# A graph network's attention layers: sums over eight tiles in a span of 72 nodes, masks made once, chains in one array

## The chip, the cores and the metric

The kernel runs on one core of one Trainium2 chip. Five engines work beside each other: TensorE (PE; its weight loads are shown as PEld), VectorE (DVE), ScalarE (ACT), GpSimd (POOL) and SyncE (SP). Each runs its own queue of instructions in order and waits for the others by semaphores. The metric is the time of one execution on the device in microseconds (us), as the median of several runs. A profile is a further execution, recorded by the hardware profiler.

## The reference

`x` has 6250 nodes of 128 values. There are 100000 edges; `dst` is sorted, and drawn as 6250 u^2 with u uniform, so low nodes have many edges and high nodes few.

```
dst = minimum((6250 * uniform(100000) ** 2.0).astype(int32), 49999);  sort by dst
h = relu(layernorm(x))
h = rgcn(h, basis1, ...); h = rgcn(h, basis2, ...)      # 16 relations, 8 bases
x = x + h
h = relu(layernorm(x))
for each of two attention layers:
    src, dst with a self loop for every node            # 106250 entries
    xw = h @ W                                          # 4 heads of 32
    e = leaky_relu(al_s[src] + al_d[dst], 0.2)
    alpha = exp(e - max over the node's entries) / (sum over the node's entries)
    out[n] = sum over the entries of n of alpha * xw[src]
    h = elu(batchnorm(out + b))
x = x + h
```

All values are float32.

## The kernel before

**Tiles.** Edges are packed with their target into sortable keys. For the attention layers the self loops are merged in (`gat_list`), which gives 106250 sorted entries, filled up to 832 tiles (NT) of 128. Eight tiles (SC) make one row of the sorted array, 1024 entries on end; 32 tiles (TC) make a chunk, and there are 26 chunks (NCH). Each entry's target node lies in `dst`, a column for each tile.

**Two relational layers** (`edge_layer`, `rgcn`) come first. They gather a row for each edge from a table in HBM, tile by tile. While the first of them runs, a generator, advanced by one step in each of 98 half groups, builds the lists of the attention layers: `gat_list`, then `windows`, then `chains`.

**Windows and passes.** A sum over the entries of a tile is a matmul with a selection: for entry e and place w of a span of nodes it has 1 where the entry's target is the span's first node plus w. `windows` stores for each tile its first node (`base`) and for each entry its distance from it (`ahead`). It also counts how many spans are needed: L353 to L357 compare the widest distance with the steps 0, W, 2W, ..., and the number of steps that aren't above it is `passes`. `layer` (L606) runs the whole attention layer in a loop of so many passes; each pass moves all spans on by W (24 nodes), through `offset` (L614) and `start` (L616). An entry that lies outside the span of a pass adds nothing in it.

**An attention layer** (`gat`, L962) goes through the chunks:

- `gathers(k + 1)`: 32 indirect DMAs from POOL's queue (L584), each with 128 rows of 136 values (128 of the node and its 8 attention values), into two row buffers of 16 tiles. The pool `grp` has 7 such buffers (L1134).
- `sums(k)`: it weights the rows in place (L917, four tiles at a time), makes a selection for every eight tiles (L601), one matmul for each tile (L937: rows as the weights, 24 columns moving), and one addition for each tile into the accumulator at a place that is read from a register (L921). Registers are loaded by `registers` (L589), 16 at a time. Ahead of it a column that two chunks share is corrected (L930, L931).
- `softmax(k + 1)`: written as a generator and woven into the steps of `sums(k)`. An edge's logit, the running maximum and the sum are taken along the 128 entries of a tile with scans (L806, L830, L831, L836, L837), with masks that say where a new node begins (`cut` L789, `same` L791). A node may go on from tile to tile, so the ends of the tiles are linked by scans over the 32 tiles of a chunk in four partitions, one for each head (L814, L852, L854, L874, L877); three values are carried over to the next chunk.

The order of each engine is that of the program text (`in_order`). Scores are turned around by PE (L799, L905), and copied by ACT (L797, L908).

**Between and after** the attention layers, `bn_elu` normalises, with tiles from the same pool `grp`, and makes the next layer's table, or the output.

Of the kernel before, what the change touches and what calls it, by code (L numbers as in the profile page):

```python
# [10 lines left out]
BF16 = mybir.dt.bfloat16  # L11
AF = mybir.ActivationFunctionType
# [32 lines left out]
NZ = -(-(N + 1) // W)  # L45
WG = 288
# [5 lines left out]
BIG = 1e30  # L52

# [14 lines left out]
class Gnn:  # L68
# [251 lines left out]
    order = staticmethod(lambda v: v.rearrange("o (c p) -> o p c", p=NP))  # L320
    by_tile = staticmethod(lambda v: v.rearrange("o (p c) -> o p c", c=SC))

    def windows(self, scratch):

        nc, const, dst = self.nc, self.const, self.dst
        order, by_tile = self.order, self.by_tile
        self.base = const.tile([1, NT], I32, name="base")
        nc.vector.tensor_copy(by_tile(self.base), order(dst[0:1, :]))  # L330
        self.ahead = const.tile([P, NT], F32, name="ahead")
        last, firsts, lasts = scratch[:, :NT], scratch[:, NT:2 * NT], scratch[:, 2 * NT:3 * NT + 1]
        flags = scratch[:, 4 * NT:6 * NT].rearrange("o (i t) -> o i t", i=2)
        for c in range(0, NT, NT // 2):
            w = slice(c, c + NT // 2)
            ps = self.ps()[:, :NT // 2]
            nc.tensor.matmul(ps, self.ones, dst[0:1, w], start=True, stop=True)
            nc.vector.scalar_tensor_tensor(self.ahead[:, w], ps, -1.0, dst[:, w], op0=ALU.mult, op1=ALU.add)
            ps = self.ps()[:, :NT // 2]
            nc.tensor.matmul(ps[:1, :], self.ident[:, P - 1:P], dst[:, w], start=True, stop=True)  # L340
            nc.vector.tensor_copy(last[:, w], ps[:1, :])
        yield
        nc.vector.tensor_copy(by_tile(firsts), order(dst[0:1, :]))
        nc.vector.memset(lasts[:, 0:1], -1.0)
        nc.vector.tensor_copy(by_tile(lasts[:, 1:]), order(last))
        nc.vector.tensor_tensor(flags[:, 0, :], firsts, lasts[:, :NT], ALU.is_equal)
        nc.vector.tensor_tensor(flags[:, 1, :], firsts, lasts[:, 1:], ALU.is_equal)

        nc.vector.tensor_sub(lasts[:, 1:], lasts[:, 1:], firsts)
        widest = scratch[:, 0:1]  # L350
        nc.vector.tensor_reduce(widest, lasts[:, 1:], AX.X, ALU.max)
        steps = self.small.tile([1, NZ], F32, name="steps", bufs=1)
        nc.vector.tensor_scalar(steps, self.steps, widest, None, op0=ALU.is_le)  # L353
        count = self.small.tile([1, 1], F32, name="count", bufs=1)
        nc.vector.tensor_reduce(count, steps, AX.X, ALU.add)
        passes = const.tile([1, 1], I32, name="passes")
        nc.vector.tensor_copy(passes, count)  # L357
        self.passes_g = passes
        yield

        self.both = const.tile([H, 2, NT], BF16, name="both")
        for i in range(2):
            for c in range(0, NT, NT // 2):
                w = slice(c, c + NT // 2)
                ps = self.ps()[:, :NT // 2]
                nc.tensor.matmul(ps[:H, :], self.ones[:, :H], flags[:, i, w], start=True, stop=True)
                nc.vector.tensor_copy(self.both[:, i, w], ps[:H, :])
        yield

    def chains(self, scratch):  # L370

        nc, const = self.nc, self.const
        chunked = lambda t: t.rearrange("h (k t) -> h k t", t=TC)
        link, one = chunked(self.both[:, 0, :]), chunked(self.both[:, 1, :])
        self.link = link
        wide = [H, NCH, TC + 1]

        self.linkpen = const.tile(wide, BF16, name="linkpen")
        nc.vector.memset(self.linkpen, -BIG)
        lk = chunked(scratch[:H, NCH * P:NCH * P + NT])  # L380
        nc.vector.tensor_scalar(lk, link, 1.0, BIG, op0=ALU.subtract, op1=ALU.mult)
        nc.vector.tensor_copy(self.linkpen[:, :, :TC], lk)
        yield


        self.through = const.tile(wide, BF16, name="through")
        nc.vector.memset(self.through, 0.0)
        nc.vector.tensor_mul(self.through[:, :, 1:], link, one)
        self.throughpen = const.tile(wide, BF16, name="throughpen")
        nc.vector.tensor_scalar(self.throughpen, self.through, 1.0, BIG, op0=ALU.subtract, op1=ALU.mult)  # L390
        yield

        self.back = const.tile(wide, BF16, name="back")
        nc.vector.memset(self.back, 0.0)
        nc.vector.tensor_mul(self.back[:, :, :TC - 1], one[:, :, :TC - 1], link[:, :, 1:])
        self.apart = const.tile([H, NCH, TC], BF16, name="apart")
        nc.vector.tensor_scalar(self.apart, one, -1.0, 1.0, op0=ALU.mult, op1=ALU.add)
        self.backpen = const.tile(wide, BF16, name="backpen")
        nc.vector.memset(self.backpen, -BIG)
        nc.vector.tensor_scalar(self.backpen[:, :, :TC], one, 1.0, BIG, op0=ALU.subtract, op1=ALU.mult)  # L400
        nc.vector.tensor_add(self.backpen[:, :, :TC - 1], self.backpen[:, :, :TC - 1], self.linkpen[:, :, 1:TC])
        yield


        self.rows = const.tile([P, NCH, P], F32, name="rows")
        ri = scratch[:, :NCH * P].bitcast(I32).rearrange("p (k e) -> p k e", e=P)
        kv = self.keys[:NT * P].rearrange("(k t e) -> t k e", t=TC, e=P)
        for h in range(H):
            nc.sync.dma_start(ri[h * TC:(h + 1) * TC], kv)
        for k in range(0, NCH, 2):  # L410
            yield
            nc.vector.tensor_scalar(ri[:, k:k + 2], ri[:, k:k + 2], KDST, None, op0=ALU.logical_shift_right)
            nc.vector.tensor_scalar_mul(self.rows[:, k:k + 2], ri[:, k:k + 2], BIG)

        self.rowlink = const.tile([P, NCH], F32, name="rowlink")
        for k in range(NCH):
            yield
            self.spread(self.rowlink[:, k:k + 1], lk[:, k, :])
# [13 lines left out]
    def own_tile(self, out, v):  # L432

        nc = self.nc
        t = self.small.tile([P, TC], F32, name="spread")
        nc.vector.tensor_mul(t, v, self.tile_of)
        nc.vector.tensor_reduce(out, t, AX.X, ALU.add)

    def spread(self, out, v):

        ps = self.ps()
        self.nc.tensor.matmul(ps[:, :TC], self.of_head, v, start=True, stop=True)
        self.own_tile(out, ps[:, :TC])
# [149 lines left out]
    def bases(self, t0):  # L593

        return self.registers(self.start[0:1, t0 // G, :])

    def selections(self, t0):

        s = self.sel.tile([P, GD, W], F32, name="sel")
        c = column(t0)  # L600
        self.nc.vector.tensor_tensor(  # L601
            s, self.window[:, None, :].to_broadcast([P, GD, W]),
            self.offset[:, c:c + (GD - 1) * NP + 1:NP, None].to_broadcast([P, GD, W]), ALU.is_equal)
        return s

    def layer(self, body):  # L606
# [3 lines left out]
        passes = nc.values_load(self.passes_g, min_val=1, max_val=NZ,  # L610
                                skip_runtime_bounds_check_because="a step of 0 is at most any width")
        self.in_order()
        with self.tc.For_i(0, passes):
            nc.vector.tensor_scalar(self.offset, self.ahead, self.moved, None, op0=ALU.subtract)  # L614
            groups = self.base.rearrange("o (g t) -> o g t", t=G)
            nc.vector.tensor_scalar(self.start, groups, self.moved[0:1, :], float(N), op0=ALU.add, op1=ALU.min)  # L616
            nc.vector.tensor_copy(self.leads, self.base[:, ::TC])
            body()
            nc.vector.tensor_scalar_add(self.moved, self.moved, float(W))
# [57 lines left out]
    def rgcn(self, acc, table, bs, wc, others=iter(())):  # L677
# [18 lines left out]
        def select(h):  # L696
            s = self.sel.tile([P, GD, W], F32, name="sel")
            nc.vector.tensor_tensor(s, self.window[:, None, :].to_broadcast([P, GD, W]),
# [78 lines left out]
    def softmax(self, k):  # L777
# [3 lines left out]

        nc, t = self.nc, lambda name: self.soft.tile([P, P], F32, name=name)
        v, carry = self.v[k], self.carry
        dr = self.rows[:, k, :]

        cut = self.soft.tile([P, P + 1], F32, name="cut")
        nc.vector.tensor_copy(cut[:, 0:1], self.rowlink[:, k:k + 1])
        nc.vector.memset(cut[:, P:], 0.0)
        nc.vector.tensor_sub(cut[:, 1:P], dr[:, :P - 1], dr[:, 1:])  # L789
        same = t("same")  # L790
        nc.vector.tensor_scalar(same, cut[:, :P], 0.0, None, op0=ALU.is_equal)  # L791
        yield
# [17 lines left out]
        dl = self.chain.tile([H, TC + 1], F32, name="dl")  # L810
        nc.vector.tensor_copy(dl[:, 1:], cps[:H, :TC])
        nc.vector.tensor_copy(dl[:, 0:1], carry[0])
        dc = self.chain.tile([H, TC + 1], F32, name="dc")
        nc.vector.tensor_tensor_scan(dc, self.through[:, k, :], dl, 0.0, op0=ALU.mult, op1=ALU.add)  # L814
        df = self.chain.tile([H, TC], F32, name="df")
        nc.vector.tensor_mul(df, dc[:, :TC], self.link[:, k, :])
# [4 lines left out]
        self.own_tile(dcol, ps[:, :TC])  # L821
        e = t("e")
        nc.vector.tensor_scalar(e, dr, dr[:, 0:1], dcol, op0=ALU.is_equal, op1=ALU.mult)
        nc.vector.tensor_add(e, e, d)
# [6 lines left out]
        nc.vector.tensor_tensor_scan(m[:, ::-1], cut[:, P:0:-1], fwd[:, ::-1], -BIG, op0=ALU.add, op1=ALU.max)  # L831
# [5 lines left out]
        nc.vector.tensor_tensor_scan(total[:, ::-1], cut[:, P:0:-1], run[:, ::-1], -BIG, op0=ALU.add, op1=ALU.max)  # L837
# [4 lines left out]
        pair = lambda x: x.rearrange("h (i t) -> h i t", i=2)  # L842

        ends = cps[:H, :4 * TC].rearrange("h (j i t) -> h j i t", j=2, i=2)
        ml = self.chain.tile([H, 2, TC + 1], F32, name="ml")
        nc.vector.tensor_copy(ml[:, 0, :TC], ends[:, 0, 0, :])
# [373 lines left out]
```

## Time and profile before

| what | us |
|---|---|
| median of 3 runs (lowest, highest) | 4508.44 (4505.27, 4509.29) |
| the profiled execution | 5581.38 |
| its span, first to last instruction | 5573.1 |
| first relational layer, first gather | 60.8 |
| second relational layer, first gather | 1302.8 |
| first attention layer, first gather | 2588.5 |
| second attention layer, first gather | 4089.2 |
| last gather | 5440.2 |
| mean granted TensorE clock | 0.613 |

The profiled execution is longer than the median run by 1073 us; durations of single instructions come from it. A busy time is the sum of an engine's instructions; idle time before an instruction is put down to what ended it. "Remote" and "another core or an unknown queue" mean that the profile doesn't show what released the wait. Gathers go through the queue `software_dynamic`, 218.57 of 256.84 MB.

### The profile page before, as it was taken

Reading aid. Unit: us, or ns where it says so; the run is one execution under the profiler, and the core shown is the slowest. Engines: PE = TensorE matmul, PEld = TensorE weight load, DVE = VectorE, ACT = ScalarE, POOL = GpSimd, SP = SyncE. Lnnn points to the kernel's source line nnn. Section 1 sums busy time; section 2 is a strip of 40 time slices with the busy share of each in tenths; the row PEclk is TensorE's granted clock in tenths of the full one; section 3 lists DMA queues with packets and bytes.
Section 4 is the critical chain, followed back from the end, with each engine's and each line's share of the span. In section 5 each row is a group of like instructions: output and inputs, shape, how many; then the busy total and the mean of one; then the engine's idle time right before and its main releaser. Section 6 shows DMA issues by size and latency. Waiting matters only on the chain.

```text
span 5573.1 us, 41706 instructions
## 1 busy us (share of the span) xinstructions
PE 2479.0 (44%) x10042; PEld 2106.2 (38%) x10042; DVE 2558.3 (46%) x8572; ACT 475.6 (9%) x683; POOL 3123.3 (56%) x3242
## 2 busy tenths in 40 slices
PE   2666666664666656663133233232412333323334
PEld 1455545553555555552123232232412322322224
DVE  4345555452444444453254444354633444444446
ACT  2011000011010000012000000000020000000002
POOL 4566666654566666633655555655246656555560
PEclk6777777785777777775555555555555555555555
DMA  3121121112122111111211111211021111111110
GB/s 102 49 55 44 45 59 46 46 36 64 50 65 55 47 46 47 47 26 48 48 41 42 39 43 40 46 38 43 17 61 44 44 39 44 42 42 42 39 44 27
DMA packets 135170, 256.84 MB, mean 46 GB/s; under 512 B 56017, under 2 KB 76485, under 8 KB 134916
## 3 DMA queue, kind: packets, MB, share of 16 engines
q0 software_dynamic: 103296, 218.57, 16.6%
q1 hardware_dynamic: 31388, 34.67, 2.0%
q8 instruction: 87, 1.43, 0.1%
q14 instruction: 167, 1.37, 0.1%
q10 hardware_dynamic: 232, 0.80, 0.1%
HBM read 236.45 MB, written 17.37 MB: 46 GB/s over the span
## 4 chain that ended last, share of the span: by engine, by line
another core or an unknown queue 24%; DVE 21%; PE 12%; issue 12%; POOL 4%; DVEq 2%; ACT 1%; DMA 0%; ACTq 0%; SPq 0%; POOLq 0%
PE ps L937 6%; POOL v L584 4%; DVE acc L921 3%; PE ps L740 2%; DVE v L917 2%; DVE part L749 2%; DVEq L589 1%; DVE own L895 1%; DVE own L900 1%; DVE den L884 1%; PE ps L711 1%; PE ps L695 1%; DVE e L901 1%; DVE hot L692 1%
## 5 line engine op out<-in xcount | busy, mean ns | idle before, releaser
L584 POOL DMA_INDIRECT v<-gtable,src_i x1664 | 1628.6, 979 | 1368.4 <-ACT sd L797 537.0
L584 POOL DMA_INDIRECT v<-htable,src_e x1564 | 1486.0, 950 | 948.8 <-issue 447.5
L740 PE MATMUL ps<-sw,v 128*128 128x192 f32 x3128 | 808.7, 423 | 213.2 <-issue 186.8
L937 PE MATMUL ps<-sel,v 128*128 128x24 f32 x3328 | 773.7, 385 | 179.3 <-DVE v L917 72.8
L937 PEld LDWEIGHTS ps<-sel,v 128*128 128x128 f32 x3328 | 748.4, 330 | 228.7 <-issue 90.8
L740 PEld LDWEIGHTS ps<-sw,v 128*128 128x128 f32 x3128 | 715.6, 255 | 270.7 <-issue 235.7
L749 DVE TENSOR_TENSOR part<-part,ps 128x192 f32 x1564 | 552.7, 353 | 362.7 <-remote 201.4
L921 DVE TENSOR_TENSOR acc<-acc,ps 128x24 f32 x1664 | 296.3, 178 | 851.2 <-remote 636.4
L711 PE MATMUL ps<-part,basis 128*128 128x288 f32 x1568 | 419.4, 422 | 7.2 <-DVE part L749 6.9
L695 PE MATMUL ps<-wc,hot 128*128 128x64 f32 x392 | 108.7, 371 | 690.4 <-DVE hot L692 642.2
L892 PE MATMUL ps<-part,of_head 4*128 4x65 f32 x104 | 35.6, 443 | 853.4 <-DVE part L890 704.5
L716 DVE TENSOR_TENSOR acc<-acc,ps 128x288 f32 x98 | 44.6, 455 | 773.4 <-remote 696.8
L706 ACT COPY part<-zero 128x2304 f32<-128x2304 f32 x100 | 210.8, 2110 | 1920.3 <-remote 1598.9
L695 PEld LDWEIGHTS ps<-wc,hot 128*128 128x128 f32 x392 | 82.4, 257 | 749.3 <-DVE hot L692 684.2
L703 DVE TENSOR_TENSOR sw<-sel,ps 128x1536 f32<-128x1536 f32 x196 | 343.7, 1754 | 25.3 <-remote 8.7
L892 PEld LDWEIGHTS ps<-part,of_head 4*128 4x128 f32 x104 | 25.8, 307 | 860.4 <-DVE part L890 709.8
L711 PEld LDWEIGHTS ps<-part,basis 128*128 128x128 f32 x1568 | 302.5, 198 | 86.2 <-issue 8.1
L430 PE MATMUL ps<-sel,head_of 128*4 128x32 f32 x208 | 44.5, 312 | 641.8 <-DVE sel L428 454.2
L917 DVE TENSOR_TENSOR v<-v,w 128x512 f32<-128x512 f32 x416 | 286.3, 688 | 8.6 <-issue 5.9
L430 PEld LDWEIGHTS ps<-sel,head_of 128*4 128x4 f32 x208 | 9.4, 84 | 654.7 <-DVE sel L428 461.4
L691 PE MATMUL ps<-relT,of_tile 8*128 8x128 f32 x392 | 122.7, 402 | 32.0 <-DMA relT<-rels 21.7
L833 ACT ACTIVATE e<-e 128x128 f32<-128x128 f32 x52 | 16.1, 309 | 1301.8 <-DVE e L832 713.4
(293 smaller groups left out, 2061.2 us busy)
## 6 DMA issues: line engine op xcount, KB each, us to landing
v<-gtable,src_i POOLq DMA_INDIRECT x1664
v<-htable,src_e POOLq DMA_INDIRECT x1564
gtable<-gtb SPq DMA_DIRECT2D x14, 476.0 KB
acc<-htable SPq DMA_DIRECT2D x24, 256.0 KB
htable<-x SPq DMA_DIRECT2D x7, 448.0 KB
relT<-rels SPq DMA_DIRECT2D x196, 4.0 KB
htable<-y SPq DMA_DIRECT2D x7, 448.0 KB
x<-in_x_dram SPq DMA_DIRECT2D x7, 441.0 KB
```

The lines of the kernel that those rows point to most:

```text
L584: self.nc.gpsimd.indirect_dma_start(out=out, out_offset=None, in_=table, in_offset=bass.IndirectOffsetOnAxis(ap=idx, axis=0))
L691: nc.tensor.matmul(ps[:, :P], self.of_tile, rel.pop(h), start=True, stop=True)
L695: nc.tensor.matmul(coef[h][:, P:P + SC * NBASE], t, wc.rearrange("p g b -> p (g b)"), start=True, stop=True)
L703: nc.vector.tensor_tensor(x, s[:, :, None, :].to_broadcast(shape), c[:, :, :, None].to_broadcast(shape), ALU.mult)
L706: nc.scalar.copy(x, self.zero[:, :, None].to_broadcast([P, NBASE, WG]))
L711: nc.tensor.matmul(ps[:, :WG], bs[:, b, :], x[:, b, :], start=b == 0, stop=b == NBASE - 1)
L740: nc.tensor.matmul(ps[:, (j - i) * NBASE * W:(j - i + 1) * NBASE * W], v[:, i0 + j, :], sw[h][:, j].rearrange("p b w -> p (b w)"), start=T ...
L749: nc.vector.tensor_add(o, o, x.rearrange("p (b w) -> p b w", b=NBASE))
L892: nc.tensor.matmul(ps[:, :2 * TC + 1], self.of_head, part, start=True, stop=True)
L917: nc.vector.tensor_mul(x, x, wz[:, :, :, None].to_broadcast([P, Q, H, FH]))
L921: nc.vector.tensor_add(o, o, ps[:, j * W:(j + 1) * W])
L937: nc.tensor.matmul(ps[:, j * W:(j + 1) * W], v[i // G][:, i % G, :D], s[:, i % GD, :], start=True, stop=True)
```

## The change

The passes' step becomes WA = 72 nodes, in place of W = 24, and a span now belongs to the eight tiles of one row (1024 entries) and not to one tile. Distances `ahead` are taken from the first node of the row, and the widest distance that sets `passes` is that of the row's last entry. The eight matmuls of a row add up in one PSUM bank (`start` at the first, `stop` at the last), and one addition of 72 columns takes them to the accumulator. Selections are 128 x 8 x 72, and rows are weighted eight tiles at a time. The relational layers keep spans of 24.

The softmax's masks `cut`, `same`, `head` and `tail` are computed for all chunks when the lists are built, and kept in bf16 and bytes. The chains' running values lie in one array `ends` of 2 x 833 for the whole pass, which the next chunk's scan takes up, and the backward ones in two arrays in turn; columns for a tile's first and last node are worked on together. One copy (`shrink`) goes from DVE to ACT. `softmax` has one step less, and isn't advanced at step 3 any longer. `grp` has 6 buffers in place of 7.

The diff, cut to its core:

```diff
+WA = 72
+NZA = -(-(N + 1) // WA)
...
     def windows(self, scratch):
+        ps = self.ps()[:, :NP]
+        nc.tensor.matmul(ps, self.ones, dst[0:1, :NP], start=True, stop=True)
+        nc.vector.tensor_sub(by_place(self.ahead), by_place(dst), ps[:, None, :].to_broadcast([P, SC, NP]))
...
-            nc.tensor.matmul(ps[:1, :], self.ident[:, P - 1:P], dst[:, w], start=True, stop=True)
+            nc.tensor.matmul(ps[:1, :], self.ident[:, P - 1:P], self.ahead[:, w], start=True, stop=True)
             nc.vector.tensor_copy(last[:, w], ps[:1, :])
+        count = self.small.tile([1, 2], F32, name="count", bufs=1)
+        nc.vector.tensor_reduce(count[:, 0:1], last, AX.X, ALU.max)
+        steps = self.small.tile([1, NZA], F32, name="steps", bufs=1)
+        nc.vector.tensor_scalar(steps, self.steps_a, count[:, 0:1], None, op0=ALU.is_le)
+        nc.vector.tensor_reduce(count[:, 1:2], steps, AX.X, ALU.add)
+        self.passes_g = const.tile([1, 1], I32, name="passes")
+        nc.vector.tensor_copy(self.passes_g, count[:, 1:2])
...
     def chains(self, scratch):
         for k in range(0, NCH, 2):
+            z = slice(k, k + 2)
...
+            nc.vector.tensor_sub(self.cut[:, z, 1:P], rows[:, z, :P - 1], rows[:, z, 1:])
+            for mask, e in ((self.head, 0), (self.tail, P - 1)):
+                nc.vector.tensor_tensor(mask[:, z], rows[:, z], rows[:, z, e:e + 1].to_broadcast([P, 2, P]), ALU.is_equal)
-        for k in range(NCH):
+        half = NCH // 2
+        for k in range(0, NCH, half):
             yield
-            self.spread(self.rowlink[:, k:k + 1], lk[:, k, :])
...
+            nc.vector.tensor_scalar(self.same[:, z], self.cut[:, z, :P], 0.0, None, op0=ALU.is_equal)
...
     def layer(self, body):
         with self.tc.For_i(0, passes):
             nc.vector.tensor_scalar(self.offset, self.ahead, self.moved, None, op0=ALU.subtract)
...
             body()
-            nc.vector.tensor_scalar_add(self.moved, self.moved, float(W))
+            nc.vector.tensor_scalar_add(self.moved, self.moved, float(WA))
...
     def softmax(self, k):
-        nc.vector.tensor_sub(cut[:, 1:P], dr[:, :P - 1], dr[:, 1:])
-        nc.vector.tensor_scalar(same, cut[:, :P], 0.0, None, op0=ALU.is_equal)
-        yield
+        cut, same = self.cut[:, k, :], self.same[:, k, :]
...
-        nc.vector.tensor_tensor_scan(dc, self.through[:, k, :], dl, 0.0, op0=ALU.mult, op1=ALU.add)
+        dc = self.ends[:, 0, :]
+        nc.vector.tensor_tensor_scan(dc[:, past], ahead, cps[:H, :TC], dc[:, k * TC:k * TC + 1], op0=ALU.mult, op1=ALU.add)
...
-        for i, c in enumerate((0, P - 1)):
-            self.own_tile(cols[:, i:i + 1], ps[:, i * TC:(i + 1) * TC])
-            nc.vector.tensor_scalar(inv, dr, dr[:, c:c + 1], cols[:, i:i + 1], op0=ALU.is_equal, op1=ALU.mult)
-            nc.vector.scalar_tensor_tensor(e, inv, 1.0, e, op0=ALU.add, op1=ALU.mult)
+        self.own_tile(cols, ps[:, :2 * TC].rearrange("p (i t) -> p i t", i=2))
+        nc.vector.tensor_scalar(inv, self.head[:, k, :], cols[:, 0:1], 1.0, op0=ALU.mult, op1=ALU.add)
+        nc.vector.scalar_tensor_tensor(inv, self.tail[:, k, :], cols[:, 1:2], inv, op0=ALU.mult, op1=ALU.add)
+        nc.vector.tensor_mul(e, e, inv)
...
     def sums(self, k, w, shrink):
-        def add(t, at, ps):
-            for j in range(2):
-                o = self.sum[:, bass.ds(at[(t + j) % G], W)]
-                nc.vector.tensor_add(o, o, ps[:, j * W:(j + 1) * W])
+        def add(i, ps):
+            o = self.sum[:, bass.ds(at[i], WA)]
+            nc.vector.tensor_add(o, o, ps[:, :WA])
...
+        at = self.registers(self.start[0:1, k, :])
...
-            ps = self.ps()
-            for j in range(2):
-                i = t + j
-                nc.tensor.matmul(ps[:, j * W:(j + 1) * W], v[i // G][:, i % G, :D], s[:, i % GD, :], start=True, stop=True)
+            for i in range(t, t + 2):
+                nc.tensor.matmul(ps[:, :WA], v[i // G][:, i % G, :D], s[:, i % GD, :],
+                                 start=i % GD == 0, stop=i % GD == GD - 1)
...
-                if step == 3 or step >= TC // 4 - 1:
+                if step >= TC // 4 - 1:
...
-        self.grp = self.pool("grp", 7)
+        self.grp = self.pool("grp", 6)
```

## The prediction

> **What bounds the kernel now.** I read the page's busy times first, then the groups of the gathers, then what POOL waited for, then POOL in order of time, then four stretches of equal work side by side.
>
> From the page (line, engine, operation, count, then busy us and mean ns):
>
> ```profile
> span 5573.1 us, 41706 instructions
> PE 2479.0 (44%) x10042; PEld 2106.2 (38%) x10042; DVE 2558.3 (46%) x8572; ACT 475.6 (9%) x683; POOL 3123.3 (56%) x3242
> ...
> L584 POOL DMA_INDIRECT v<-gtable,src_i x1664 | 1628.6, 979 | 1368.4 <-ACT sd L797 537.0
> L584 POOL DMA_INDIRECT v<-htable,src_e x1564 | 1486.0, 950 | 948.8 <-issue 447.5
> ```
>
> POOL does nothing but gathers, and is busier than any other engine. The 1664 gathers of the attention layers are 2 x 832: one for each of the 832 tiles in each layer, so each layer's loop ran once. The attention loop's first instruction says so too:
>
> ```profile
> L614 DVE TENSOR_SCALAR offset<-ahead,moved x2: 653/653/653, 2585.2 to 4085.7; 128x832 f32<-128x832 f32 x2
> ```
>
> POOL in order of time, at the end of one run of gathers (start, duration, idle before):
>
> ```profile
> 3077.85 0.94 POOL L584 DMA_INDIRECT v<-gtable,src_i  x1 [0.30 <-issue]
> 3079.10 0.94 POOL L584 DMA_INDIRECT v<-gtable,src_i  x1 [0.30 <-issue]
> 3095.22 1.22 POOL L584 DMA_INDIRECT v<-gtable,src_i  x1 [15.18 <-ACT sd L797]
> 3096.74 0.94 POOL L584 DMA_INDIRECT v<-gtable,src_i  x1 [0.30 <-issue]
> ```
>
> A gather starts every 1.25 us, 40 us for the 32 tiles of a chunk; then, in the profiled execution, POOL waits some 13 to 15 us for a free row buffer. The last table sets two chunks with gathers beside two at the end of the layer without (us, busy time and count of PE, PEld, DVE, ACT, POOL, then clock, DMA share, GB/s):
>
> ```profile
> 3691.80:3744.40 52.60, 17.22 (x77) 15.75 (x76) 24.52 (x108) 1.83 (x8) 31.55 (x32) 0.50 0.19 43
> 3744.40:3797.30 52.90, 17.23 (x77) 15.76 (x77) 24.53 (x108) 1.84 (x8) 31.24 (x32) 0.50 0.19 43
> 3962.60:3991.90 29.30, 17.30 (x77) 15.83 (x77) 24.12 (x108) 1.88 (x8) 0.00 (x0) 0.50 0.00 0
> 3991.90:4021.30 29.40, 17.29 (x77) 15.75 (x77) 24.04 (x108) 1.83 (x8) 0.00 (x0) 0.50 0.00 1
> ```
>
> The same work of DVE and PE takes 29.3 us with POOL quiet and 52.8 us beside gathers, with the same busy times: the difference is waiting.
>
> **Which of these holds in the runs shown.** The profiled execution took 5581 us (span 5573, 8 around it), the median run 4508. I try the gathers alone. Busy 1628.6 + 1486.0, plus 3228 gaps of 0.30, makes 4083 us. In five stretches of the profile POOL has no gather at all: 61 before the first, 83 between the relational layers, 144 ahead of each attention layer and 132 at the end (the wait and idle columns of POOL and the first and last starts of L584), 564 together. 4083 + 564 leaves 926 of the span for waits between gathers. The median run is 1073 below the profiled one. So it has no room for those waits: 4508 - 8 - 4083 = 417 remain for the five stretches, less than their 564. That fits if the layers' ends don't lag as they do here (the last gather of the first attention pass starts at 3944 and its last addition ends at 4039). With ends of about 440 the interval comes to 1.26 us. I take the unprofiled kernel to be paced by the gathers throughout, at 1.26 us each, with DVE and PE hidden below them. This is an inference; the second and third rivals are what follows if it is false.
>
> **The change, part by part.**
>
> *The number of passes.* This decides. A pass adds only edges whose node lies within the span after its start; the loop runs once for every step 0, span, 2 x span ... that isn't above the widest reach. Before, the reach is that of one tile of 128 sorted entries, and the span 24. After, it is that of eight tiles, 1024 entries, and the span 72. Targets are 6250 u^2, so near node n there are 100000 / (2 sqrt(6250 n)) edges a node and one self loop: 9 at the last node. 128 / 9 is 14 nodes, 1024 / 9 is 114. Worked out exactly on the reference's inputs, the widest tile reaches 17 and the widest group 113; 44 of the 104 groups reach 72 or more. 17 is below 24: one pass. 113 is above 72 and below 144: steps 0 and 72 count, so *two passes*, in each of the two attention layers. The body is all inside that loop: 832 gathers, 26 chunks of softmax, the weighting and the sums are done again. The second pass costs at least 832 x 1.26 = 1048 us on POOL. Around it lies a tail in which POOL is idle: landing and softmax of the last chunk, then its sums. The profile has 29.3 us for a chunk without gathers and 17 from the last chunk's weights at 4021.3 to its last addition; less what can start before the last landing (some 10) and what DVE saves below, some 35, and 5 to restart the loop (at 4085.2 to 4089.2 in the profile). I take 40; the ends are 25 and the lagging 94. One more pass: 1088. Two layers: *+2176 us*.
>
> *Sums.* For a chunk, 32 additions at 0.178 become 4 of 128x72, between 0.178 and the 0.29 of a 128x128 one; I take 0.24: -4.7 us. The 4 selections grow from 128x192 (0.35) to 128x576; the 128x512 weighting took 0.69, so 0.75: +1.6. The 8 weightings (5.5) become 4 twice as long (estimate 1.25 each): -0.5. Two register loads, of 16 and one, become one of five: -2 on DVE's queue. PE still runs 32 matmuls, each in two parts, 72 columns wide; rows of 24 and 192 columns take 385 and 423 ns, so nothing.
>
> *Softmax.* Masks computed once take away L787 to L791 (0.73); one array for the chains takes away the copies and memsets of L811, L812, L846 to L849 and L873 to L880 (1.1); the two-fold column work (L436, L437, L900, L901: 2.0) and L823, L824, L888, L890 shrink by about 1.3; the copy L903 goes to ACT, which is busy 1.8 of 52 us. Together some -3. So DVE goes from 24.3 to about 17.5 us a chunk. Beside 40 us of gathers that is worth nothing on the path; without that cover it would be 26 x 7 = 180 us a pass. Only the tails keep it: about -8 for each of the two passes that were there, *-15*.
>
> *Lists.* Cut, head, tail and same are made once, in 15 steps in place of 39: a subtraction and two comparisons of 256 elements for each of 13 (about 0.35 each by the 128x192 row, 14 us), two long comparisons (4), less 26 column spreads of two 0.18 operations (9). +9 on DVE in the first relational layer, where gathers pace it and DVE is busy 77 of 139 us at most: nothing; 9 if uncovered.
>
> *Row buffers, 7 to 6.* A chunk holds two. A gather three chunks ahead now waits for the same half of chunk k to be summed, in place of a half before it; behind it on POOL's queue stand all later gathers, and behind those the next softmax on ACT, PE and DVE. With a chunk of 40 us on POOL and under 29 on DVE, POOL doesn't run ahead and finds buffers free: nothing. In the normalisation stages the same pool serves three tiles a step: 0 to 20 us over both; I take 5.
>
> *Two rules weighed.* The Trainium skill (DMA: Bandwidth & Descriptors, section Anatomy of one DMA) gives a DMA of this kind 2.0 us plus its bytes at 436 GB/s; 128 rows of 544 B make 2.16 us. If gathers stood one after another, the added 1664 would cost 3594 and the sum would be 8080. The trace has one every 1.25 us, since several are in flight; I use the row. The second speaks against the change's longer DVE operations: the skill (SBUF — State Buffer, section Who interferes with whom) says that a DVE operation with two SBUF inputs makes a GpSimd operation that reads SBUF wait for its whole length. The new selections and weightings are 0.7 to 1.25 us long. Taken fully, 8 us a chunk would be added, 830 over four passes, and 7490 in all. The trace has such operations now, 6.9 us a chunk, and its gathers average 978 ns over a median of 945: 1.1 us a chunk. So scaled, 8 us cost 0.2 more: 5 a pass, inside the range.
>
> *Sum.* 4508 + 2176 - 15 + 5 = 6674; I say **6670**, 48% slower. Against the profiled execution's own time: old passes took 1454 (2585.2 to 4038.9) and 1440; a new one lies between 1090 and 1440, so its profile should have 5581 + 2 x 1447 - 4 x (0 to 357), 7050 to 8480, far above the median run as now.
>
> **Rivals.** (1) *One pass after all*: the place is the widest group's reach, and it decides at 72; with 71 or less the loop would run once, and the change would save its two tails and little else: about 4490, faster by 0.4%. The measure of 113 speaks against it. (2) *The old kernel was paced by DVE and PE, and the profiler slows all alike* (4508 / 5581 = 0.81): gathers every 1.02 us, the old pass 1170 or 45 a chunk. The new chunk then falls to about 37 (45 less 7 and a few waits), the pass to 26 x 37 + 40 = 1002: 4508 - 2340 + 4008 = 6180. For it: the 15 us waits of POOL. Against it: it needs gathers a fifth faster than any in the trace. (3) *Delays beside gathers stay*, as 52.8 against 29.3 shows, and the new pass runs at some 45 a chunk: 4508 + 2 x (1170 + 40) = 6930. (4) The change does what it says, and DVE's gain shows: it would need passes under half the old one's, below about 560; the gathers' busy time alone is 814 a pass.
>
> **How the numbers follow.** Paced by gathers, two passes: 0.72, own range 6560 to 6760. Rival 2: 0.13. Rival 3: 0.13. Rival 1: 0.02. The range 6420 to 6800 takes in the tails of 25 to 94, intervals down to 1.15, and parts of rivals 2 and 3. About 0.2% is what a measurement of this kernel can tell from no change. Slower 0.98, faster 0.015, same 0.005.
>
> **What would show it.** In the changed kernel's profile: 3328 gathers from gtable in place of 1664; the offset instruction of the loop 4 times; 6656 records of the summing matmul; 416 additions of 128x72; DVE's busy time a chunk near 17.5 us; chunks without gathers near 22 us at the ends of passes. The prediction is wrong if the offset instruction appears twice (rival 1), or if gathers in the new kernel stand much closer than 1.25 us (rival 2), or if its unprofiled time can't be met by 4892 gathers at 1.26 plus some 500 (rival 3).

## The result, and the profile after

The changed kernel takes 6735.9 us (median of 4 runs, 6728.2 to 6738.7), the kernel before 4507.1 beside it (4505.3 to 4509.3): a ratio of 1.494 [1.492, 1.497], 49% slower. Forecast were 6670 and a range of 6420 to 6800. The profiled execution of the changed kernel took 6738.7 us with a span of 6736.9.

The experiments ran on four chips, and the kernel before took 4505 us on one of them (the shorter kind below, as in the runs of the result) and 5447 to 5650 on the three others (the longer kind), so every experiment is read beside a run of it on the same chip; the profile of before that the prediction used (5581) is of the longer kind, the profile after of the shorter.

From the page after (engines' busy us, share and instructions; then groups with count, busy us, mean ns of one, and the idle time before them):

```profile
span 6736.9 us, 52453 instructions
PE 3583.0 (53%) x13892; PEld 2852.6 (42%) x13892; DVE 3276.6 (49%) x8958; ACT 590.5 (9%) x1152; POOL 4805.5 (71%) x4907
...
L586 POOL DMA_INDIRECT v<-gtable,src_i x3328 | 3309.0, 994 | 1277.5 <-issue 1193.0
L586 POOL DMA_INDIRECT v<-htable,src_e x1564 | 1487.7, 951 | 567.3 <-issue 450.0
```

The attention layers' gathers are doubled, the relational layers' 1564 are not. The loop's first instruction, seen by its source line, has four executions:

```profile
L611 DVE TENSOR_SCALAR offset<-ahead,moved x4: 652/653/654, 2161.7 to 5570.1; 128x832 f32<-128x832 f32 x4
```

POOL in order of time where the first pass ends and the second begins (start, duration, idle before it):

```profile
3246.71 0.94 POOL L586 DMA_INDIRECT v<-gtable,src_i  x1 [0.30 <-issue]
3285.92 0.94 POOL L586 DMA_INDIRECT v<-gtable,src_i  x1 [38.27 <-DVE start L614]
```

The four passes' first gathers start at 2165.0, 3285.9, 4451.0 and 5571.1. A pass and its tail thus take 1120.9 and 1120.1 us, where 1088 was forecast; the tail of 39.2 (3246.7 to 3285.9, forecast 40) is in it.

Two chunks with gathers, and that tail (busy us and count of PE, PEld, DVE, ACT, POOL, then clock, DMA share, GB/s):

```profile
3385.70:3427.10 41.40, 18.11 (x77) 15.86 (x77) 19.04 (x57) 2.03 (x9) 31.65 (x33) 0.50 0.24 54
3427.10:3468.40 41.30, 18.02 (x77) 15.76 (x77) 19.05 (x57) 2.02 (x9) 31.55 (x33) 0.50 0.24 55
3246.70:3285.90 39.20, 24.86 (x107) 22.60 (x107) 20.34 (x63) 1.71 (x7) 0.94 (x1) 0.50 0.04 5
```

DVE fell from 24.5 us and 108 instructions a chunk to 19.05 and 57. The chunk now takes 41.3 us, which is 32 gathers of 0.994 with 0.30 between them. POOL never waits inside a pass: its longest idle time between two gathers of one pass is 0.31 us. In this profile the gathers set the pace.

### The profile page after: what moved, and what is told of

The parts are those of the page before. It is cut to its first block, busy times and chain, and to the rows that moved or that the text cites. A ratio compares the mean times of both kernels' runs of the same rounds, so it can differ in the third digit from the quotient of the medians.

```text
span 6736.9 us, 52453 instructions
## 1 busy us (share of the span) xinstructions
PE 3583.0 (53%) x13892; PEld 2852.6 (42%) x13892; DVE 3276.6 (49%) x8958; ACT 590.5 (9%) x1152; POOL 4805.5 (71%) x4907
## 5 line engine op out<-in xcount | busy, mean ns | idle before, releaser
L586 POOL DMA_INDIRECT v<-gtable,src_i x3328 | 3309.0, 994 | 1277.5 <-issue 1193.0
L913 PE MATMUL ps<-selg,v 128*128 128x72 f32 x6656 | 1581.7, 423 | 179.8 <-DVE v L899 176.5
L913 PEld LDWEIGHTS ps<-selg,v 128*128 128x128 f32 x6656 | 1486.1, 330 | 272.8 <-DVE v L899 197.2
L738 PE MATMUL ps<-sw,v 128*128 128x192 f32 x3128 | 901.1, 417 | 286.3 <-DMA v<-htable,src_e 256.2
L738 PEld LDWEIGHTS ps<-sw,v 128*128 128x128 f32 x3128 | 583.4, 225 | 555.2 <-DMA v<-htable,src_e 269.3
L709 PE MATMUL ps<-part,basis 128*128 128x288 f32 x1568 | 547.0, 517 | 2.5 <-DVE part L747 2.5
L899 DVE TENSOR_TENSOR v<-v,w 128x1024 f32<-128x1024 f32 x416 | 507.9, 1221 | 22.1 <-DMA v<-gtable,src_i 16.3
L792 ACT COPY sd<-v 128x64 f32<-128x64 f32 x416 | 106.6, 302 | 2610.0 <-DMA v<-gtable,src_i 2610.0
L598 DVE TENSOR_TENSOR selg<-window,offset 128x576 f32<-128x576 f32 x416 | 317.7, 764 | 0.0
L902 DVE TENSOR_TENSOR acc<-acc,ps 128x72 f32 x416 | 93.8, 225 | 272.7 <-PE ps L913 272.7
```

What stands on the lines that cost most here:

```text
L586: self.nc.gpsimd.indirect_dma_start(out=out, out_offset=None, in_=table, in_offset=bass.IndirectOffsetOnAxis(ap=idx, axis=0))
L598: self.nc.vector.tensor_tensor(s, self.window[:, None, :].to_broadcast([P, GD, WA]), self.offset[:, g:g + (GD - 1) * NP + 1:NP, None].to_b ...
L709: nc.tensor.matmul(ps[:, :WG], bs[:, b, :], x[:, b, :], start=b == 0, stop=b == NBASE - 1)
L738: nc.tensor.matmul(ps[:, (j - i) * NBASE * W:(j - i + 1) * NBASE * W], v[:, i0 + j, :], sw[h][:, j].rearrange("p b w -> p (b w)"), start=T ...
L792: nc.scalar.copy(st[:, :, z * G:(z + 1) * G], v[z][:, :, D + i * H:D + (i + 1) * H].rearrange("p t h -> p h t"))
L899: nc.vector.tensor_mul(x, x, wz[:, :, :, None].to_broadcast([P, GD, H, FH]))
```

## The experiments

Ratios are to the kernel before, run on the same chip. The expectations of the first four kernels were written in absolute times of the shorter kind; their chip turned out to be of the longer one.

**One pass.** Everything of the change but the second pass: the span reaches the widest group (113). Selections and additions grow with it, to 114 columns for each group.

```diff
-WA = 72
+WA = 114
```

> The changed kernel with a span of 114 nodes in place of 72, so that the widest group of 113 fits and the loop runs once. Theory (the second pass of gathers is the whole loss): 832 gathers of the attention table in each layer, 6736 - 2 x 1121 = 4494, so 4450 to 4530, within 1% of the kernel before. Rival (the layout by eight tiles costs time in itself, by its longer DVE operations): clearly above 4600. Rival (DVE and PE paced the old kernel, and their lighter work now shows): 4300 or less.

Measured: 5216 us (5202 to 5240) against 5551, a ratio of 0.938 [0.933, 0.943]. Without its second pass the change gains 6% on this chip. What the second pass costs is measured by the pair further down, where both forms ran on one chip.

**The kernel before, once more.** No edit; beside it on the same chip are its untraced runs.

> The kernel before, unchanged, profiled once more. Theory (paced by gathers in its usual runs; the long profiled execution was delayed by something that isn't there in these): if the execution takes about 4507, a gather every 1.25 to 1.31 us without pauses, 40 to 42 us a chunk, and gaps of some 40 to 55 us less in the stretches between layers than before. Rival (DVE and PE paced it): chunks of about 45 us with POOL waiting 5 us or more in each.

Measured: 5547 us profiled, 5551 untraced. So the profiler doesn't make the time longer, and the 1.60 to 1.62 us from gather to gather, with 260 to 275 us of POOL's waits in a pass, don't come from it. They belong to the longer kind.

**The old body, made to run twice.** The old kernel's attention span of 24 is cut to 12, below its widest reach of 17:

```diff
+WB = 12
...
-        nc.vector.tensor_scalar(steps, self.steps, widest, None, op0=ALU.is_le)
+        nc.vector.tensor_scalar(steps, self.steps, WB / W, widest, op0=ALU.mult, op1=ALU.is_le)
```

(the selections, the sums and the loop's step follow WB).

> The kernel before with the attention spans cut from 24 to 12 nodes, so that its loop runs twice, with the old sums and the old softmax. Theory (a pass costs its gathers, whatever DVE does): two more passes at about 1075 plus an end of 50, so 6700 to 6790, as the changed kernel within 1%. Rival (the change's lighter DVE work shortens a pass): clearly longer than the changed kernel, by up to 4 passes x 26 chunks x 7 us = 730, about 7400.

Measured: 8594 us, 3043 above the kernel before on that chip, 1522 a pass. The loop's first instruction in this kernel, by its source line:

```profile
L615 DVE TENSOR_SCALAR offset<-ahead,moved x4: 652/652/654, 2588.1 to 7068.0; 128x832 f32<-128x832 f32 x4
```

Four passes again, with none of the change's other parts: a span below the reach doubles the passes of the old body too. The absolute expectation was missed, since a pass is longer on this kind of chip.

**More gathers.** In the changed kernel every fourth gather is made twice, into the same rows; 832 more in all:

```diff
+                if i % 4 == 0:
+                    self.gather(self.v[k][i // G][:, i % G, :], table, self.src_i[:, c:c + 1])
```

> The changed kernel with every fourth gather of the attention layers made twice: 8 more a chunk, 832 over the four passes, the same rows to the same place. Theory (paced by gathers at 1.25 to 1.30 us): 1040 to 1080 more, 7780 to 7820. Rival (paced by DVE and PE, or by a latency in each pass): POOL has room, less than 300 more.

Measured: 9555 us. Against the changed kernel on a chip of the same kind (7755, next experiment) that is 1800 more, 2.16 for each; the two chips differ by 1.3% in the kernel before, so this is rough. The group of gathers on its page:

```profile
L586 POOL DMA_INDIRECT v<-gtable,src_i x4160 | 4085.7, 982 | 2946.8 <-DMA v<-gtable,src_i 1524.3
```

1524 of the idle time ended with the landing of a gather: the repeat writes the rows that the first is still writing, and waits 1.83 us for it (1524 / 832). So this run doesn't measure the price of an added gather. POOL got some 2490 us more (714 of gathers, 250 of gaps, 1524 of these waits), and the kernel 1800: most of it shows, and the rest fell into waits that POOL has on this kind of chip anyway.

**The changed kernel and its one-pass form, side by side.** On one chip of the longer kind; the second has the edit of the first experiment.

> The changed kernel, unchanged, beside the other kernels of this batch. Theory (a pass costs its gathers where nothing delays them, and the old pass's delayed length where waits stay): if the kernel before takes about 4507 here, 6736; if it takes about 5551, two more passes of 1220 to 1300 us and shorter first ones, 7500 to 7900.

> The changed kernel with a span of 114 nodes, one pass in each attention layer, once more. Theory: where the kernel before takes about 4507, the gathers pace both: 4480 to 4560, within 1%, the longer selections making gathers a little longer. Where it takes about 5551, about 5216 again. Rival (the lighter DVE work counts in any case): faster by 3% or more also beside 4507.

Measured: 7755 (7742 to 7769), ratio 1.379 [1.370, 1.388], and 5211 (5191 to 5220), ratio 0.926 [0.921, 0.931]. One constant makes 2544 us, 1272 for each pass taken away. In the first one's trace the second passes start 1256 and 1280 after the first ones. The waits of DVE in that trace (total us, times, longest us), and then those of the changed kernel's profile shown above:

```profile
DVE acc L902 <- remote: 1919.1, 133, 30.6
```

```profile
DVE acc L902 <- PE ps L913: 272.7, 212, 3.2
```

The busy times of both are alike (gathers 1013 and 994 ns, DVE 3285.6 and 3276.6 us in all), and so is the granted clock in the attention layers (0.50). What differs is how long the addition waits, 1919 us in 133 long waits for which the profile names no releaser, and with it the chunk: 46.8 against 41.3 us. The first of the two traces in order of time shows what is late (start, duration, idle before):

```profile
3202.65 5.97 PE L913 MATMUL ps<-selg,v 128*128 128x72 f32 x27
...
3208.84 0.97 PE L913 MATMUL ps<-selg,v 128*128 128x72 f32 x4
...
3214.14 0.23 DVE L902 TENSOR_TENSOR acc<-acc,ps 128x72 f32 x1 [8.48 <-remote]
...
3229.04 0.23 DVE L902 TENSOR_TENSOR acc<-acc,ps 128x72 f32 x1 [12.87 <-remote]
...
3230.29 0.26 PE L437 MATMUL ps<-sel,head_of 128*4 128x32 f32 x2 [20.48 <-DVE sel L435]
```

The two additions take up groups of matmuls that ended at 3205.2 and 3208.6, so PE had been done for 8.9 and 20.4 us. Over the whole trace, 1904 of the additions' 2137 us of waiting come after the last matmul of their group; an addition that waited starts 6.0 us after it as median and at most 39.7. In the changed kernel's profile of the shorter kind that is 0.04 us every time. The trace also has the updates of PE's semaphore for which the additions wait: from 3210.5 to 3229.0 they come 0.7 to 2.9 us apart, though the last matmul ended at 3209.8, and each addition starts 0.02 us after one of them. So the time is lost between PE's end and the signal of it, nearly all of it beside gathers (2098 of the 2137 us). Why the signals are late on these chips isn't shown; their traces also hold only a part of them (4950 of 6322 updates of that semaphore here, all in the shorter kind), which would explain why a releaser is often missing.

**One SBUF input.** The weightings take their weights, and the selections their window, from PSUM, so that neither has two SBUF inputs. Two PSUM banks are kept for that, and the general pool falls from 8 to 6:

```diff
-        self.psum = pool("psum", 8, space=bass.MemoryType.PSUM)
+        self.psum = pool("psum", 6, space=bass.MemoryType.PSUM)
+        self.kept = pool("kept", 1, space=bass.MemoryType.PSUM)
...
-            s, self.window[:, None, :].to_broadcast([P, GD, WA]),
+            s, self.wwin[:, None, :].to_broadcast([P, GD, WA]),
...
-        w = self.soft.tile([P, H, TC], F32, name="w")
-        nc.scalar.copy(w.rearrange("p h t -> p (h t)"), ps[:, :P])
+        w = ps[:, :P].rearrange("p (h t) -> p h t", h=H)
...
+        self.wwin = self.kept.tile([P, 512], F32, name="wwin")[:, :WA]
+        nc.vector.tensor_copy(self.wwin, self.window)
```

> The changed kernel with the edges' weights and the window's numbers read from PSUM, so that the weighting and the selection have one SBUF input each in place of two; the copy of the weights to SBUF falls away. Theory (long DVE operations with two SBUF inputs hold up gathers: 167 us over the four passes, 156 of them beside the weighting): the mean gather falls from 994 ns to 945 to 960, and the time by 110 to 165 us against the changed kernel of this batch where gathers pace it. Rival (gathers are long for another reason, such as traffic in HBM): mean gather as it was, within 20 us of the changed kernel.

> Both edits: one pass with a span of 114, and one SBUF input for weighting and selection. Theory: gathers at 1.25 us without lengthening, 1664 of them: 50 to 90 us below the one-pass kernel of this batch, and below the kernel before. Rival (gathers are long for another reason): as the one-pass kernel, within 20 us.

Same chip as the pair above. The gathers by their source line (minimum, median, longest ns), of the changed kernel and then of this one:

```profile
L586 POOL DMA_INDIRECT v<-gtable,src_i x3328: 939/945/2006, 2579.5 to 7644.2; - x196
```

```profile
L587 POOL DMA_INDIRECT v<-gtable,src_i x3328: 938/945/1132, 2725.5 to 8077.7; - x196
```

The mean falls from 1013 to 947 ns and the longest from 2006 to 1132: DVE's two-input operations do lengthen gathers. (The two missing banks don't shorten them: in the next experiment, with these operations as they were, the mean is 1038.) The time goes the other way, which neither theory had: 8177 us with two passes (ratio 1.454 [1.447, 1.462], 422 more than the unedited kernel) and 5509 with one (0.981 [0.975, 0.986], 298 more). A part of it lies where no selection or weighting runs at all: the first attention gather comes 146 us later, and in the second relational layer there is one gather every 1.571 us, in place of 1.461. Of this edit only the missing banks reach there.

**Six banks alone.** The one-pass form with the smaller pool and nothing else. This batch ran on a chip of the shorter kind.

> The one-pass kernel (span 114) with the PSUM pool cut from 8 to 6 banks and nothing else, to set the two edits of the one-input kernels apart. Theory: where the kernel before takes about 5551 to 5625, the two banks are what made the one-input kernel lose, so about 5500 to 5600 (300 to 380 above the one-pass kernel with 8 banks), with gathers as long as before at 1024 ns. Rival (the one SBUF input itself costs, by PSUM reads): 5190 to 5240. Where the kernel before takes about 4507, gathers pace it and banks don't matter: 4480 to 4580.

Measured: 4563.8 us (4561.6 to 4567.4) against 4505.2, 1.3% slower: ratio 1.0129 [1.0112, 1.0146]. Here the second relational layer kept its 1.254 us a gather, so on such a chip the banks cost them nothing, and the run doesn't part banks from inputs in the attention layers. It answers another question: what is left of the change when its second pass is gone. From its page:

```profile
L586 POOL DMA_INDIRECT v<-gtable,src_i x1664 | 1727.8, 1038 | 691.3 <-issue 582.8
```

With selections of 128x912 (1.11 us each, in place of 0.76 for 128x576) the gathers are longer still, 1038 ns, one every 1.343. Against the 1.30 that is worked out below for the kernel before, it is an estimated 1664 x 0.043 = 72 us, where 59 were measured; the 13 between them weren't traced. What six banks add in the attention layers isn't known.

**DVE's saving given back.** The changed kernel with 24 copies of 128x128 a chunk on DVE, inside the softmax:

```diff
+        for z in range(24):
+            nc.vector.tensor_scalar_mul(inv, e, 1.0)
```

> The changed kernel with 24 copies of 128x128 added to each chunk's softmax on DVE, about 7 us, which is what the change takes off DVE. Theory: where the kernel before takes about 4507, gathers hide it: 6736 plus 0 to 60 (an end of each of four passes, 7 us each, and some longer gathers). Where it takes about 5551 to 5625, waits of DVE lie on the path: 100 to 800 above 7755. Rival (DVE paces a pass in any case): 4 x 26 x 7 = 730 more in both.

On the same chip: 6824.9 us (6824.0 to 6825.8), ratio 1.515 [1.512, 1.518], 89 above the 6735.9 of the result (the kernel before differs by 2 us between the two). Its copies, and its gathers:

```profile
L887 DVE TENSOR_SCALAR own<-e 128x128 f32<-128x128 f32 x2496 | 685.1, 274 | 86.0
...
L586 POOL DMA_INDIRECT v<-gtable,src_i x3328 | 3381.6, 1016 | 1290.8 <-issue 1173.7
```

685 us more on DVE cost 89, a little above the 0 to 60 that was expected. Of these 89, 73 are the gathers' own lengthening: 22 ns each, 3328 times. The other 16 lie at the ends of passes, where no gather covers DVE: POOL's idle time between two passes of a layer is 43.1 and 43.2 us in place of 38.3 and 38.7. So beside gathers DVE's time is free here, except for what lengthens the gathers. Some copies were long too (median 227 ns, longest 449); whether the same thing held them up wasn't traced.

**One input, eight banks as long as the relational layers run.** The one-pass form with one SBUF input; the pool of 8 is closed after the relational layers, and 6 and 2 banks are taken from there on:

```diff
+        self.early.close()
+        self.psum = self.pool("psum2", 6, space=bass.MemoryType.PSUM)
+        self.kept = self.pool("kept", 1, space=bass.MemoryType.PSUM)
```

> One pass (span 114) and one SBUF input for weighting and selection, with 8 PSUM banks kept for the relational layers and 6 for the attention layers only. Theory: where the kernel before takes about 4507, gathers of 947 ns in place of 1038 take 1664 x 0.09 = 150 us off the one-pass kernel's 4564: 4400 to 4450, faster than the kernel before by 1 to 2%. Where it takes about 5551 to 5625, the relational layers are back at their old length, and only the attention layers wait longer: 5250 to 5450. Rival (gathers' length is not what paces the attention layers): 4540 or more beside 4507.

> The kernel before, profiled in this batch. Theory: where it takes about 4507, one gather every 1.26 to 1.30 us without pauses, chunks of 40 to 42 us, mean gather of 960 to 990 ns, waits of POOL between gathers under 60 us in all, and ends as short as the changed kernel's. Where it takes about 5551: as in the first profile, 52 us a chunk. Rival (DVE and PE pace it at 4507): chunks of 43 us or more with POOL waiting in each.

The chip was of the longer kind: 5284.5 us (5271.6 to 5286.5) against 5487.1, ratio 0.962 [0.958, 0.965]. The second relational layer is back at 1.447 us a gather (1.452 in the kernel before on this chip), so its loss was the banks. The attention layers stay at 1.517, with gathers of 948 ns. By ratio this is behind the plain one-pass form (0.926 and 0.938). The kernel before, profiled on this chip, took 5446.8, with 226 us of POOL's waits in a pass (284 to 290 in its first profile). What this version does on a chip of the shorter kind, where gathers set the pace and 90 ns less on each of 1664 would be 150 us below the 4564, wasn't run; nor were six banks and PSUM reads parted in the attention layers.

## Why the prediction was right, point by point

*The number of passes.* Right, and it decides the result. Four offset instructions, 3328 gathers; the old body with too small a span pays for a second pass likewise, and the changed one with a span of 114 gets rid of it. The reach of 113, worked out from the reference's inputs, decided.

*The length of a pass.* Right in its mechanism, with one term mis-sized. The tail of 40 measured 39.2. The interval of 1.26 us, from "With ends of about 440 the interval comes to 1.26 us", measured 1.30 (1081.7 us over 831 intervals in the first pass). It was off in two ways. The stretches without any gather are some 375 us in the profile after, not 440: of the 2165.0 us up to the first attention gather, 200 remain beside 1564 relational gathers at 1.256, then come 88 between the layers and 87 at the end. And the average covered two kinds: relational gathers take 1.256, attention gathers 1.30. The kernel before, with the same stages around it, leaves (4507 - 8 - 2165 - 88 - 87) / 2 = 1080 for one of its runs of gathers, 1.30 each; this is worked out, since no profile of it on a chip of the shorter kind was taken. Its attention row, 979 + 300 ns, would have given 1.28, about half of the way. Two passes at 1120.5 in place of 1088 are 65 us, and the miss is 66.

*Where luck came in.* The sum starts from 4508, so it speaks of the shorter kind, and the result was measured there. On a chip of the longer kind the same change gave a ratio of 1.379, and the forecast range, 6420 to 6800 over 4508, begins at 1.42. That the shorter kind has no waits between gathers was inferred, and the profile after bears it out for the changed kernel.

*The small terms.* 4507 + 2 x 1120.5 is 6748; the 6736 measured leave -12 for tails, buffers and lists, against the -10 forecast. Single terms among them weren't measured, but the row buffers cost nothing between gathers, as expected: POOL doesn't wait there.

*DVE's work.* The additions (0.225 against 0.24), selections (0.766 against 0.75) and weightings (1.22 against 1.25) are as costed; the softmax lost less, so that a chunk has 19.05 us and not 17.5. It matters little: 6.6 us a chunk put back cost 16 us in all, beside the longer gathers.

*The two rules weighed.* Of the rule on two SBUF inputs the direction is shown: of SBUF — State Buffer, section Who interferes with whom, the Trainium skill's statement that such operations hold up a GpSimd operation reading SBUF agrees with 1013 against 947 ns. Its size was between the two that were weighed. In the first profile a gather's mean is 33 ns above the median, 1.1 us a chunk. The changed kernel has 68 ns on a chip of the same kind, 2.2 us, and 50 ns in the profile after, 1.6 us. The 0.5 to 1.1 added are more than the 0.2 scaled from the row, and far from the 8 of the full rule. The estimate of 2.16 us for one gather isn't a pace, as the prediction held: in the profile after a gather lands 2.6 us after its issue, and the next one starts after 1.30. (From their own terms the two sums come to 8092 and 7500, in place of 8080 and 7490; nothing rests on them.)

*The changed kernel's own profile.* Wrong: 7050 to 8480 was forecast, far above the median run, and it took 6739. The step took the first profile's waits for something that profiling brings. They go with the chip: on the chip of the pair above the changed kernel took 7755, inside that range.

*The rivals.* One pass needs a span of 114 on these inputs; with it the ratio was 0.93 to 0.94 on chips of the longer kind and 1.013 (with six banks) on the shorter, where the rival had 4490. An old kernel paced by DVE and PE, with gathers a fifth faster than any seen: no trace has a median interval below 1.249, and on the shorter kind the one-pass form, with less work on DVE, wasn't faster. The old kernel itself wasn't profiled there. Delays that stay beside gathers: not in the profile after, where POOL doesn't wait inside a pass; on the other chips they are there, and there the ratio is 1.379. DVE's gain on the path: not where gathers set the pace; on the longer chips the one-pass form gains, and whether by DVE's shorter work or by fewer waits wasn't parted.

## What to carry to other kernels

When a span, window or block is widened and a loop's count depends on the data, count the loop's passes from the data first: here 44 of 104 groups reached 72 or more, and that alone outweighed every instruction saved. A repeated pass costs the bound engine's work over again; here the work saved on an engine beside it wasn't set against that. Take the pace of the bound engine from the row of that very stage, not from an average over stages with different rows, and ask whether the change makes that row longer. Where a wait has no named releaser, look when the producer's last instruction ended: it tells a slow producer from a late signal.

## What the runs showed of the hardware that was not expected

- The same program takes 4505 us on one chip and 5447 to 5650 on three others. Busy times are alike; on the longer ones an engine's signal reaches the engine that waits for it late, nearly always beside gathers: 1904 of 2137 us of the additions' waiting come after PE was done, and 787 of 807 us in the first profile of the kernel before. Why wasn't settled, nor whether it is the chip itself, for each batch of runs had another chip. It changes which kernel is better: the one-pass form is 6 to 7% faster than the kernel before on the longer chips, its six-bank form 1.3% slower on the shorter.
- DVE operations of 0.76 to 1.22 us with two SBUF inputs made the gathers beside them 7% longer (947 to 1013 ns on one chip). Short copies with one input made them 2% longer (994 to 1016, on chips of the shorter kind); the Trainium skill's section named above counts that operation among those that can take both ports.
- Two PSUM banks fewer cost the second relational layer 0.11 us a gather on a chip of the longer kind (1.461 to 1.571), and nothing on the shorter (1.254).
